# A fused RWKV and mixture-of-experts block: products of ones at the start, first rows on two queues, later lookups and more buffers for results

## The chip, the core and the metric

The kernel runs on one core of a Trainium2 chip. A core has a matrix engine (PE), a vector engine (DVE), a scalar engine (ACT), a general engine (POOL), and a queue of its own for transfers (SP). ACT and POOL can start transfers too. Each engine takes its instructions strictly in program order and waits on semaphores for what the others produce; the on-chip memory has 128 partitions. The metric is the device time in microseconds (us) of one execution, as a median of several.

## The reference

Input is `x` of shape (2, 2048, 256). What is computed, all in float32:

```
xn  = layernorm(x)                                  # over the last axis, 256 wide
# attention: a decaying sum over time, per channel
k, v = xn @ key_w.T, xn @ value_w.T                 # k does not enter the recurrence
r    = sigmoid(xn @ recep_w.T)
att  = (r * wkv_scan(time_decay, time_first, v)) @ out_w.T
# mixture of experts: 8 experts, the best 2 of each row, and one shared expert
scores = softmax(xn @ gate_w.T + gate_b);  top 2 of 8
expert(e) = (silu(xn @ w1[e].T + b1[e]) * (xn @ w3[e].T + b3[e])) @ w2[e].T + b2[e]
y = sum over the two experts of a row of score * expert
z = (silu(xn @ ws1.T + bs1) * (xn @ ws3.T + bs3)) @ ws2.T + bs2   # shared, 512 wide inside
out = x + att + y + z
```

There are 4096 rows, so 8192 pairs of a row and an expert.

## The kernel before

The 4096 rows are 8 chunks of 512 rows, each of 4 groups of 128. Chunks are taken in the order `ORDER` = 2, 3, 0, 1, 4 (`FIRST`), then 5, 6, 7 (`LAST`). The work has four stages.

1. **Rows in.** `load_flow` (L428) issues on SP the rows of each chunk, the weights `ws13` of the shared expert in two halves (after the first and third chunk, `WHEN`), and then the other weights. `norm_flow` (L485) normalizes: statistics on DVE (L495, L497), the power on POOL (L500, L501), then the even groups on DVE (L507), the odd ones with a shift from DVE (L511) on ACT (L515). `turn_flow` (L519) transposes the rows on PE (L530), ACT copies them out, and PE makes the gate scores (L552, L562).
2. **Routing.** `route_flow` (L578) finds on DVE the two experts of each row and the place of each pair in a sorted list. `scatter_flow` (L733) then writes the rows to `xs_d` in that order, with 64 indirect transfers on POOL (L744), paced by the products of PE.
3. **Experts.** The sorted list is 66 tiles of 128 pairs: 50 taken two at a time with one expert (`double_flow`, L1257), 7 single ones, and 9 mixed ones that hold up to four experts in quarters (`tile_flow`, L1169). Their order is `SEQ`, sorted from the numbers in `PLACE` (L210). `rows_flow` (L1131) loads the sorted rows on SP and transposes them on DVE. `goes_flow` (L1154) loads 2 numbers for each pair of 8 tiles from `xs_d` (`meta`, L1161) and makes of them, with two small DVE operations (L1165, L1166), the places `goes` to which the results belong. `store` (L1242) writes the results to `ys_d` by indirect transfers on POOL.
4. **Results back.** When all tiles are stored, `collect_flow` (L1320) loads for each group the two results of its rows (`y`, 32 loads of 256 KB on SP, three buffers), and `combine_flow` (L1331) adds them with their scores on DVE (L1338). The sums of a chunk start as `x` (`base_flow`, L965) plus the bias `bs2` (`bias_sum_flow`, L975, an add of 128x1024 on DVE at L980). `out_flow` (L1368) writes them out.

Beside these stages PE has work that can be put where there is room: the hidden layer of the shared expert (`hidden_flow`, L930, products at L951), the attention's projections (L883) and their last products (`dense_flow`, L1002, products at L1020). Hidden layers of the last chunks are held back (L935) and fill the time in which the results come back.

The order on every engine is written by a planner when the program is built (`Plan`, L84). Each flow is a generator that yields the engine and a length in ns that it asks for (`on`, L177), a pause, or an event to wait for. The planner takes the request that can start first; among those within 150 ns of each other on one engine, it takes the lower rank. `Room` counts free buffers: `U` is a pool of 32 buffers of 2 KB a partition (`NU`), `KEEP` and `MORE` are how many of them a hidden layer has to leave free, `X` three buffers for the sums, `Y` the three for `y`. `land` (L398) is the planner's model of a transfer. On the chip, the engines follow the planned order, whatever the real times are.

Of the kernel before, what the change touches and what calls it, by code (L numbers as in the profile page):

```python
# [208 lines left out]

PLACE = {j: j / 2 for j in range(0, DBL, 2)}  # L210
PLACE |= {j: 6.1 + 2.1 * (j - DBL) for j in range(DBL, UNI)}
PLACE |= {j: 5.5 + 2 * (j - UNI) for j in range(UNI, TILES)}
SEQ = sorted(PLACE, key=PLACE.get)
assert sorted(SEQ) == [*range(0, DBL, 2), *range(DBL, TILES)]
AT = {j: n for n, j in enumerate(SEQ)}
# [9 lines left out]

PIECES = (((0,), (1,), (2,), (3,)), ((0, 1), (2, 3)))
NU = 32
KEEP = 3

FIRST, LAST = (2, 3, 0, 1, 4), (5, 6, 7)  # L230
ORDER = FIRST + LAST

HALVES = [(FIRST[0], i) for i in range(2)]

WHEN = (0, 2)

PACE = 4000

# [1 line left out]

LATE = 1000

BETWEEN = (2, 4)

EAGER = 6
MORE = 8

AHEAD = [(LAST[0], i) for i in range(2)]

# [4 lines left out]
def rwkv_moe_kernel(  # L254
# [33 lines left out]
    ROWS, H, YS = Room(plan, 2), Room(plan, 3), Room(plan, 3)  # L288

    PH, HP, PO = (Room(plan, n) for n in (4, 2, 2))  # L290
    XST, SIS, HST, Y = Room(plan, 3), Room(plan, 2), Room(plan, 2), Room(plan, 3)

    STILL = Room(plan, 3)
    STATS, MIX, XSM = Room(plan, 3), Room(plan, 1), Room(plan, 1)
# [57 lines left out]
    goes = fixed([P, TILES], "goes", I32)  # L352

    def constants():
        make_identity(nc, ident)
        nc.gpsimd.memset(zero, 0.0)
        nc.gpsimd.memset(neg_half, -0.5)
        nc.gpsimd.memset(ones, 1.0)

        nc.gpsimd.memset(before, 1.0)  # L360
        nc.gpsimd.affine_select(
            out=before, in_=before, pattern=[[1, P]], compare_op=ALU.is_gt, fill=0.0, base=0, channel_multiplier=-1
        )

        for e in range(E):
            nc.gpsimd.memset(rev[:, e : e + 1], float(E - e))

        for q in range(P // Q):
            nc.gpsimd.iota(
                starts[ts(q, Q)], pattern=[[P, TILES]], base=q * Q, channel_multiplier=0,  # L370
                allow_small_or_imprecise_dtypes=True,
            )
        nc.gpsimd.memset(wg[:, :, E:], 0.0)
        nc.gpsimd.memset(st_pp, -10000.0)
        nc.gpsimd.memset(st_bb, 0.0)
        nc.gpsimd.memset(st_aa, 0.0)


    loaded = {}
    have = {n: event() for n in ("vec", "wg", ("ws13", 0), ("ws13", 1), "ws2", "bs2", "wa", "x", "cleared", "we", "bias_d", "bias", "routed", "tiles")}  # L380
    normed = {(c, n): event() for c in range(NCH) for n in range(NT)}
    turned = {c: event() for c in range(NCH)}
    half_turned = [event() for _ in range(2)]
# [14 lines left out]
    def land(nbytes, then, *rooms):  # L398


        def flow():
            yield on(nbytes / 370, "Q")
            yield 2000
            for e in then:
                e.set()
            for r in rooms:
                r.give()

        plan.add(flow(), 0)

    def number_flow(c):
# [3 lines left out]
            allow_small_or_imprecise_dtypes=True,  # L415
        )

    def small_load_flow():

        for to, of in (  # L420
            (vec, vecs), (bg, b_gate.partition_broadcast(P)),
            (wg[:, :, :E], w_gate.rearrange("p (k e) -> p k e", k=NC)),
        ):
            yield on(600, "ACT")
            nc.scalar.dma_start(to, of)
        land(P * (NV * 4 + 64), [have["vec"], have["wg"]])

    def load_flow():  # L428
        for i, c in enumerate(ORDER):
            side = "left" if c in LEFT else "right"  # L430
            xn[c] = p_early[side].tile([P, NT, R], F32, tag=f"xn{c}", name=f"xn_{c}")
            for groups in PIECES[i > 0]:
                n, m = groups[0], len(groups)
                yield on(300 + 100 * m, "SP")
                nc.sync.dma_start(xn[c][:, n : n + m, :C], rows(x, c)[:, n : n + m, :])
                loaded[c, n] = event()
                plan.add(norm_flow(c, groups), 1 + i / 10)
                land(P * m * C * 4, [loaded[c, n]])
            plan.add(number_flow(c), 2)
            if i in WHEN:  # L440
                n = WHEN.index(i)
                of = slice(n * SI // 2, (n + 1) * SI // 2)
                yield on(600, "SP")
                nc.sync.dma_start(
                    ws13[:, :, :, of], w_sh13.rearrange("p (m k i) -> p m k i", m=2, k=NC)[:, :, :, of]
                )
                land(P * 4096, [have["ws13", n]])
        land(0, [have["x"]])
        yield on(500, "SP")
        nc.sync.dma_start(ws2, w_sh2.rearrange("p (k d) -> p k d", k=NSI))  # L450
        land(P * 4096, [have["ws2"]])
        yield on(500, "SP")
        nc.sync.dma_start(bs2, b_out[E, :].partition_broadcast(P))
        land(P * 1024, [have["bs2"]])
        for n, name in enumerate(("wv", "wr", "wo")):
            yield on(500, "SP")
            nc.sync.dma_start(wa[name], w_attn[n].rearrange("p (k d) -> p k d", k=NC))
        land(3 * P * 2048, [have["wa"]])

# [273 lines left out]
    def scatter_flow():  # L733
# [4 lines left out]
        for side, chunks in (("left", LEFT), ("right", RIGHT)):  # L738
# [27 lines left out]
        yield LATE  # L766
# [4 lines left out]
            flow = still_flow if j < DBL else one_flow if j < UNI else quarters_flow  # L771
            plan.add(flow(j), (9 if j < DBL else 15) + AT[j] / 100)
        for j in range(0, TILES, GO):
            plan.add(goes_flow(j), 10 + j / 100)
        plan.add(collect_flow(), 3)


# [152 lines left out]
    def hidden_flow(c, i):  # L930

        if (c, i) not in HALVES:
            yield turned[c]
        yield have["ws13", i // 2]
        if c in LAST and (c, i) not in AHEAD:  # L935
            yield turn[SEQ[-6]]
        pts = []
# [37 lines left out]
    def bias_sum_flow(c):  # L975
        t = sums[c]
        yield have["bs2"]
        yield have["routed"]
        yield on(1250, "DVE")
        nc.vector.tensor_tensor(  # L980
            t, t, bs2.unsqueeze(1).to_broadcast([P, NT, C]), ALU.add
        )
        sum_ready[c].set()
# [147 lines left out]
    def rows_flow(j):  # L1131
# [19 lines left out]
        turned_rows[j] = xT  # L1151
        rows_in[j].set()

    def goes_flow(j):  # L1154

        for c in range(NCH):
            yield scattered[c]
        n = min(GO, TILES - j)
        yield on(400, "SP")
        where = xs_d[j * P : (j + n) * P, R_TO:].rearrange("(n p) c -> p n c", p=P)  # L1160
        nc.sync.dma_start(meta[:, j : j + n, :], where)  # L1161
        yield 4000
        yield on(320, "DVE")
        to, top = meta[:, j : j + n, 0], meta[:, j : j + n, 1]
        nc.vector.tensor_tensor(top, top, likes[:, j : j + n], ALU.is_equal)  # L1165
# [154 lines left out]
    def collect_flow():  # L1320

        yield have["tiles"]
        for c in DONE:
            for n in range(NT):
                g = c * NT + n
                yield on(420, "SP", (Y, 1))
                y = late["ys"].tile([P, 2, C], F32, tag="ys", name=f"y_{g}")
                nc.sync.dma_start(y, ys_d[2 * g * P : 2 * (g + 1) * P, :].rearrange("(p w) c -> p w c", w=2))
                plan.add(combine_flow(c, n, y), 4)

    def combine_flow(c, n, y):  # L1331
# [1 line left out]
        yield 2000  # L1333
        yield sum_ready[c] if c in LAST else resumed[c]
        g = c * NT + n
        yield on(960, "DVE")
        for w in range(2):
            nc.vector.scalar_tensor_tensor(  # L1338
                sums[c][:, n, :], y[:, 1 - w, :], score[w][:, g : g + 1], sums[c][:, n, :], ALU.mult, ALU.add
            )  # L1340
        Y.give()
        step_done(c, n, closing[c, n // 2])

    def step_done(c, n, done):
# [40 lines left out]
            closing[c, half] = {"pe": pe, "sum": 0, "of": 2 + (c in LAST), "then": leaves(c, half)}  # L1385

    constants()
    plan.add(small_load_flow(), 0)
    plan.add(load_flow(), 0)
    for i, c in enumerate(ORDER):  # L1390
        plan.add(turn_flow(c), 1 + i / 10)
        if c in FIRST:
# [101 lines left out]
```

## Time and profile before

| | |
|---|---|
| median of 3 runs | 470.21 us (469.22 to 470.86) |
| the profiled execution | 469.83 us, of which the span is 468.1 us |
| mean granted clock of PE in the profiled execution | 0.992 |
| DVE, ACT, POOL busy | 360.5 us (77%), 195.4 us (42%), 192.4 us (41%) |
| loads of `y`, of `meta`, indirect stores to `ys_d` | 32, 9, 66 |

The span runs from the first to the last instruction of the program; 1.7 us lie around it. "Busy" counts the time in which an instruction of the engine is under way. For PE the page says itself that the ends of products are modelled and that a busy PE is not PE at its peak. The lists in order of time have start, length, engine, line, operation, output and inputs, how many instructions were merged, and in brackets the idle time ahead with what ended it.

### The profile page before, as it was taken

The page shows a single profiled execution, that of the slowest core. Times are in us where ns is not written, and L with a number is a line of the kernel's source. Part 1 is how long each engine was busy: PE and PEld are TensorE (multiplying, and loading weights), DVE is VectorE, ACT ScalarE, POOL GpSimd, SP SyncE. Part 2 cuts the span into 40 slices and gives each one's busy share as a digit, 9 for nine tenths or more (in the row PEclk, how much of TensorE's full clock was granted, in tenths as well). Part 3 has the DMA queues.
Part 4 walks back from the last instruction along what each step waited for, and adds up shares of the span by engine and source line. Part 5 has one row for each costly group of instructions (what it writes and reads, how often), then busy time and mean ns, then how long its engine had stood idle before and what let it go on. Part 6 is the DMA issues. An engine that isn't in the chain of part 4 may idle for free.

```text
span 468.1 us, 6776 instructions
## 1 busy us (share of the span) xinstructions
PE 449.2 (96%) x1965; PEld 295.2 (63%) x1965; DVE 360.5 (77%) x722; ACT 195.4 (42%) x383; POOL 192.4 (41%) x228
## 2 busy tenths in 40 slices
PE   4999999999999988999999999999999999999994
PEld 2755556444686556866676656667667576445883
DVE  4776999979678468986897789476559777786876
ACT  3777210261140316436934683734877245112000
POOL 6650047777777012365435444464452432200000
PEclk9999999999999998999999999999999999999998
DMA  7999922475253885477736585666685400278885
GB/s 230 365 269 193 281 73 82 139 243 182 102 177 109 225 159 153 153 205 215 177 106 193 166 235 168 194 163 201 175 263 135 151 17 34 91 215 297 264 286 174
DMA packets 90980, 84.93 MB, mean 181 GB/s; under 512 B 50429, under 2 KB 76318, under 8 KB 90816
## 3 DMA queue, kind: packets, MB, share of 16 engines
q1 hardware_dynamic: 82432, 62.24, 47.2%
q0 software_dynamic: 7952, 22.23, 15.2%
q8 instruction: 16, 0.26, 0.2%
q14 instruction: 20, 0.16, 0.1%
q10 hardware_dynamic: 560, 0.04, 0.1%
HBM read 44.93 MB, written 26.70 MB: 153 GB/s over the span
## 4 chain that ended last, share of the span: by engine, by line
PE 72%; DVE 11%; DMA 10%; SPq 3%; issue 3%; DVEq 0%; ACT 0%
PE ph L1285 16%; PE p L951 15%; PE pos L1308 9%; PE po L1020 9%; DMA y<-ys_d 6%; PE wvp L883 6%; PE wrp L883 4%; PE ph L1183 3%; PE ph L1187 3%; DVE pa L1338 2%; PE pos L1225 2%; PE tp L530 2%; DVE si L960 1%; DMA xs<-xs_d 1%; SPq L1143 1%
## 5 line engine op out<-in xcount | busy, mean ns | idle before, releaser
L1247 POOL DMA_INDIRECT ys_d<-ys,goes x66 | 75.6, 1146 | 141.1 <-DVE ys L1315 45.0
L951 PE MATMUL p<-xnT,ws 128*128 128x512 f32 (+1 forms) x272 | 116.7, 576 | 0.0
L1285 PE MATMUL ph<-xsT,still 128*128 128x256 f32 x400 | 93.3, 381 | 0.9 <-DMA xs<-xs_d 0.9
L744 POOL DMA_INDIRECT xs_d<-xn,slot x64 | 68.8, 1075 | 49.1 <-DVE eq L690 29.9
L951 PEld LDWEIGHTS p<-xnT,ws 128*128 128x128 f32 x272 | 51.9, 195 | 53.2 <-issue 49.6
L1285 PEld LDWEIGHTS ph<-xsT,still 128*128 128x128 f32 x400 | 74.7, 190 | 14.8 <-issue 5.2
L1020 PE MATMUL po<-ws,si 128*128 128x256 f32 x256 | 59.3, 379 | 1.1 <-DVE si L960 1.1
L1020 PEld LDWEIGHTS po<-ws,si 128*128 128x128 f32 x256 | 48.6, 190 | 11.1 <-issue 2.6
L1308 PE MATMUL pos<-we,si 128*128 x200 | 50.0, 395 | 3.3 <-DVE si L1298 2.1
L1308 PEld LDWEIGHTS pos<-we,si 128*128 128x128 f32 x200 | 37.8, 195 | 19.7 <-issue 5.6
L957 ACT ACTIVATE si<-p,vec 128x512 f32<-128x512 f32 x32 | 21.7, 685 | 56.3 <-PE p L951 56.2
L1119 ACT COPY own<-we 128x512 f32 x72 | 40.2, 621 | 1.0 <-issue 0.9
L1147 DVE STREAM_TRANSPOSE xsT<-xs 128x512 f32<-128x512 f32 (+1 forms) x41 | 24.5, 600 | 16.7 <-DMA xs<-xs_d 15.7
L911 ACT ACTIVATE th<-wrp 128x512 f32<-128x512 f32 x16 | 9.5, 596 | 66.3 <-PE wrp L883 61.8
L1271 ACT ACTIVATE si<-ph,bcol 128x256 f32<-128x256 f32 x50 | 21.0, 471 | 32.4 <-PE ph L1285 30.3
L1298 DVE SCALAR_TENSOR_TENSOR si<-ph,bcol,si 128x256 f32<-128x256 f32 x50 | 21.6, 473 | 15.1 <-PE ph L1285 14.6
L1020 PE MATMUL po<-wo,rw 128*128 128x256 f32 x128 | 31.9, 379 | 0.0
L883 PE MATMUL wrp<-xnT,wr 128*128 128x512 f32 x64 | 30.1, 592 | 0.0
L883 PE MATMUL wvp<-xnT,wv 128*128 128x512 f32 x64 | 29.1, 595 | 0.0
L1020 PEld LDWEIGHTS po<-wo,rw 128*128 128x128 f32 x128 | 24.3, 190 | 5.0 <-issue 1.9
L864 DVE RECIPROCAL bb<-bb 128x512 f32<-128x512 f32 x8 | 26.8, 3353 | 0.3
L1315 DVE TENSOR_TENSOR ys<-pos,b 128x512 f32<-128x512 f32 x25 | 17.2, 686 | 12.1 <-PE pos L1308 11.7
(158 smaller groups left out, 592.5 us busy)
## 6 DMA issues: line engine op xcount, KB each, us to landing
still<-we SPq DMA_DIRECT2D x25, 512.0 KB
y<-ys_d SPq DMA_DIRECT2D x32, 256.0 KB
xs<-xs_d SPq DMA_DIRECT2D x100, 64.0 KB
we<-in_w_exp_dram SPq DMA_DIRECT2D x16, 256.0 KB
xb<-in_x_dram SPq DMA_DIRECT2D x8, 512.0 KB
pa<-part_d SPq DMA_DIRECT2D x8, 512.0 KB
xn<-in_x_dram SPq DMA_DIRECT2D x14, 256.0 KB
part_d<-xb SPq DMA_DIRECT2D x5, 512.0 KB
```

The costliest lines, as they stand in the source:

```text
L744: step = nc.gpsimd.indirect_dma_start(out=xs_views[2 * g + w], out_offset=bass.IndirectOffsetOnAxis(ap=slot[w][:, g : g + 1], axis=0), in_ ...
L864: nc.vector.reciprocal(den, den)
L883: nc.tensor.matmul(pt, wa[name][:, k, ts(ch, P)], xnT[c][k], start=(k == 0), stop=(k == NC - 1))
L951: nc.tensor.matmul(pts[m][:, of], ws13[:, m, k, ts(i, P)], xnT[c][k][:, of], start=(k == 0), stop=(k == NC - 1))
L957: nc.scalar.activation(si, pts[0], AF.Silu, bias=vec[:, V_BS1 + i : V_BS1 + i + 1])
L1020: nc.tensor.matmul(po[:, j, :], l[:, ts(2 * half + j, P)], r, start=(i == 0), stop=(i == len(parts) - 1))
L1119: nc.scalar.copy(mine[q, k], we[:, which[j, q], 0:2, k, :])
L1147: nc.vector.transpose(xT.rearrange("p k (b t) -> p b k t", t=Q), t.rearrange("p b (k i) -> p b k i", i=Q))
L1247: nc.gpsimd.indirect_dma_start(out=ys_views[j], out_offset=bass.IndirectOffsetOnAxis(ap=goes[:, j : j + 1], axis=0), in_=y, in_offset=None ...
L1285: nc.tensor.matmul(p[m][:, i, :], mine[k][:, m, ts(i, P)], xT[:, k, :], start=(k == 0), stop=(k == NC - 1))
L1298: nc.vector.scalar_tensor_tensor(si[:, i, :], p[1][:, i, :], mine["b"][:, 1, i : i + 1], si[:, i, :], ALU.add, ALU.mult)
L1308: nc.tensor.matmul(po[:, t, :], si[:, i, ts(t, P)], we[:, e, 2, i, :], start=(i == 0), stop=(i == NI - 1))
```

## The change

The changed places are named after what they do. Before the first rows arrive, PE multiplies a tile of ones by itself 20 times (`warm_flow`). Of the first chunk's rows, groups 1 and 3 are issued from ACT ahead of the small loads, groups 0 and 2 from SP. `ws13` comes in quarters: after the first chunk, after the second, and two after the third. The planner's model of a transfer goes from 370 bytes per ns and 2000 ns to 330 and 2200. `goes_flow` waits for a tile that lies `SOON` = 8 tiles ahead of the first that needs the lookup, if there is such a tile, and leaves 8000 instead of 4000 ns for the transfer. The bias sums of chunks 2, 3, 5, 6, 7 go from DVE to POOL, and those of 2 and 3 no longer wait for the routing. `y` has five buffers instead of three, taken from the pool `U`, and its adds have rank 45 instead of 4. `KEEP`, `BETWEEN`, `EAGER` and `PLACE` get other numbers.

```diff
-PLACE |= {j: 5.5 + 2 * (j - UNI) for j in range(UNI, TILES)}
+PLACE |= {j: 5 + 2 * (j - UNI) for j in range(UNI, TILES)}
...
-KEEP = 3
+KEEP = 2
...
-WHEN = (0, 2)
+WHEN = (0, 1, 2, 2)
...
-BETWEEN = (2, 4)
-EAGER = 6
+BETWEEN = (2,)
+EAGER = 7
...
+ASIDE = FIRST[:2] + LAST
+WARM = 20
+SOON = 8
+BACK = 5
...
-    XST, SIS, HST, Y = Room(plan, 3), Room(plan, 2), Room(plan, 2), Room(plan, 3)
+    XST, SIS, HST, Y = Room(plan, 3), Room(plan, 2), Room(plan, 2), Room(plan, BACK)
...
     def constants():
+        nc.gpsimd.memset(ones, 1.0)
         make_identity(nc, ident)
...
-        nc.gpsimd.memset(ones, 1.0)
...
-            yield on(nbytes / 370, "Q")
-            yield 2000
+            yield on(nbytes / 330, "Q")
+            yield 2200
...
+    def x_load(engine, c, groups, i):
+        n, m = groups[0], len(groups)
+        engine.dma_start(xn[c][:, n : n + m, :C], rows(x, c)[:, n : n + m, :])
+        loaded[c, n] = event()
+        plan.add(norm_flow(c, groups), 1 + i / 10 + n / 100)
+        land(P * m * C * 4, [loaded[c, n]])
+
+    def warm_flow():
+        yield 600
+        yield on(3800, "PE", (PS, 1))
+        t = bank([P, P], "warm")
+        for n in range(WARM):
+            nc.tensor.matmul(t, ones, ones, start=True, stop=True)
+        PS.give()
+
     def small_load_flow():
+        for n in range(1, NT, 2):
+            yield on(450, "ACT")
+            x_load(nc.scalar, ORDER[0], (n,), 0)
...
             for groups in PIECES[i > 0]:
-                n, m = groups[0], len(groups)
-                yield on(300 + 100 * m, "SP")
-                nc.sync.dma_start(xn[c][:, n : n + m, :C], rows(x, c)[:, n : n + m, :])
-                loaded[c, n] = event()
-                plan.add(norm_flow(c, groups), 1 + i / 10)
-                land(P * m * C * 4, [loaded[c, n]])
+                if i or groups[0] % 2 == 0:
+                    yield on(400 + 75 * len(groups), "SP")
+                    x_load(nc.sync, c, groups, i)
             plan.add(number_flow(c), 2)
             if i in WHEN:
-                n = WHEN.index(i)
-                of = slice(n * SI // 2, (n + 1) * SI // 2)
+                n, m = WHEN.index(i), WHEN.count(i)
+                of = slice(n * P, (n + m) * P)
...
-            plan.add(goes_flow(j), 10 + j / 100)
+            plan.add(goes_flow(j), 10 + needed(j) / 100)
...
-        yield have["ws13", i // 2]
+        yield have["ws13", i]
...
         yield have["bs2"]
-        yield have["routed"]
-        yield on(1250, "DVE")
-        nc.vector.tensor_tensor(
+        aside = c in ASIDE
+        if not aside:
+            yield have["routed"]
+        yield on(*((2300, "POOL") if aside else (1250, "DVE")))
+        (nc.gpsimd if aside else nc.vector).tensor_tensor(
             t, t, bs2.unsqueeze(1).to_broadcast([P, NT, C]), ALU.add
         )
...
+    def needed(j):
+        return min(AT[i if i in AT else i - 1] for i in range(j, min(j + GO, TILES)))
+
     def goes_flow(j):
...
+        if needed(j) >= SOON:
+            yield turn[SEQ[needed(j) - SOON]]
...
-        yield 4000
+        yield 8000
...
-                yield on(420, "SP", (Y, 1))
-                y = late["ys"].tile([P, 2, C], F32, tag="ys", name=f"y_{g}")
+                yield on(420, "SP", (Y, 1), (U, 1))
+                y = u([P, 2, C], f"y_{g}")
...
-        yield on(960, "DVE")
+        yield on(960, "DVE", rank=45)
...
         Y.give()
+        U.give()
...
+    rows_tile(ORDER[0])
+    plan.add(warm_flow(), 0)
+    plan.add(load_flow(), 0)
     plan.add(small_load_flow(), 0)
-    plan.add(load_flow(), 0)
```

(`rows_tile` makes the tile `xn` of a chunk, as `load_flow` did.)

More of the change, by code (lines that the diff above doesn't have):

```diff
@@ L379, in rwkv_moe_kernel @@
     loaded = {}
-    have = {n: event() for n in ("vec", "wg", ("ws13", 0), ("ws13", 1), "ws2", "bs2", "wa", "x", "cleared", "we", "bias_d", "bias", "routed", "tiles")}
+    have = {n: event() for n in ("vec", "wg", *(("ws13", i) for i in range(NSI)), "ws2", "bs2", "wa", "x", "cleared", "we", "bias_d", "bias", "routed", "tiles")}
     normed = {(c, n): event() for c in range(NCH) for n in range(NT)}
@@ L416, in number_flow, with rows_tile @@
         )
+    def rows_tile(c):
+        side = "left" if c in LEFT else "right"
+        xn[c] = p_early[side].tile([P, NT, R], F32, tag=f"xn{c}", name=f"xn_{c}")
+    def x_load(engine, c, groups, i):
[11 more added lines that the diff above has]
+        PS.give()
     def small_load_flow():
+        for n in range(1, NT, 2):
+            yield on(450, "ACT")
+            x_load(nc.scalar, ORDER[0], (n,), 0)
         for to, of in (
@@ L429, in load_flow @@
         for i, c in enumerate(ORDER):
-            side = "left" if c in LEFT else "right"
-            xn[c] = p_early[side].tile([P, NT, R], F32, tag=f"xn{c}", name=f"xn_{c}")
+            if i:
+                rows_tile(c)
             for groups in PIECES[i > 0]:
-                n, m = groups[0], len(groups)
-                yield on(300 + 100 * m, "SP")
-                nc.sync.dma_start(xn[c][:, n : n + m, :C], rows(x, c)[:, n : n + m, :])
-                loaded[c, n] = event()
-                plan.add(norm_flow(c, groups), 1 + i / 10)
-                land(P * m * C * 4, [loaded[c, n]])
+                if i or groups[0] % 2 == 0:
+                    yield on(400 + 75 * len(groups), "SP")
+                    x_load(nc.sync, c, groups, i)
             plan.add(number_flow(c), 2)
             if i in WHEN:
-                n = WHEN.index(i)
-                of = slice(n * SI // 2, (n + 1) * SI // 2)
+                n, m = WHEN.index(i), WHEN.count(i)
+                of = slice(n * P, (n + m) * P)
                 yield on(600, "SP")
@@ L446, in load_flow @@
                 )
-                land(P * 4096, [have["ws13", n]])
+                land(m * P * 2048, [have["ws13", n + q] for q in range(m)])
         land(0, [have["x"]])
```

## The prediction, made before the changed kernel was run

> **What bounds the kernel now.** The busy shares and the 40 slices of the page come first.
>
> ```profile
> PE 449.2 (96%) x1965; PEld 295.2 (63%) x1965; DVE 360.5 (77%) x722; ACT 195.4 (42%) x383; POOL 192.4 (41%) x228
> ...
> PE   4999999999999988999999999999999999999994
> ```
>
> PE is the bound: no other engine reaches 80%, and the chain that ended last is 72% PE. The products are the same after the change, so time can be won only where PE stands still or runs slowly: the low digits at the start, near slices 14 and 15 (164 to 187 us), and at the end. I read the order of time in those places.
>
> ```profile
> 5.68 0.69 PE L530 MATMUL tp<-ident,xn 128*128 128x128 f32 x2 [5.68 <-DVE xn L507]
> ...
> 8.38 2.07 PE L951 MATMUL p<-xnT,ws 128*128 128x256 f32 x4
> ...
> 18.90 1.89 PE L951 MATMUL p<-xnT,ws 128*128 128x256 f32 x8
> ```
>
> **Start.** PE begins at 5.68. Four 256-wide products take 2.07 us at 8.38, but eight take 1.89 at 18.90: 0.43 each against 0.215 (less some 0.17 for the last one's end). Full pace comes at about 12.9, after some 4.5 us of steady work, though the granted clock reads 1.00. The table of 2 us stretches gives 9.23 us of busy PE in the first 16 us. Idle are 6.8; the half pace costs 10 products x 0.215 = 2.1, and about 1.2 on the transposes. So 10.1 us are lost there.
>
> ```profile
> 9.05 0.75 DVE L495 BATCH_NORM_STATS2 stats<-xn 128x6 f32<-128x256 f32 x2 [1.95 <-DMA xn<-in_x_dram]
> 9.72 0.30 DVE L497 BATCH_NORM_AGGREGATE mv<-stats 128x2 f32<-128x6 f32 x2
> 9.94 0.12 DVE L511 SCALAR_TENSOR_TENSOR shift<-mv,rstd 128x1 f32<-128x1 f32 x1
> ```
>
> Here DVE waits 1.95 us for the second chunk's rows while the last shift of the first chunk, all of whose inputs are there, stands behind it; ACT and PE wait for that shift until 10.76.
>
> **First experts.** PE has run out of other work when the first tiles come.
>
> ```profile
> 166.03 0.17 DVE L1165 TENSOR_TENSOR meta<-meta,likes 128x8 f32<-128x8 f32 x1 [0.66 <-DMA meta<-xs_d]
> ...
> 167.66 1.97 PE L1308 MATMUL pos<-we,si 128*128 x8 [1.04 <-issue]
> ...
> 174.02 0.16 DVE L1165 TENSOR_TENSOR meta<-meta,likes 128x2 f32<-128x2 f32 x1 [0.98 <-issue]
> ...
> 176.94 3.63 PE L1308 MATMUL pos<-we,si 128*128 x8 [2.14 <-DVE si L1298]
> ```
>
> All nine lookups are issued between 158 and 170, and DVE takes them in line: it waits for their transfers and so reaches the product `si` (L1298) late, which PE needs. PE idles 1.04 and 2.14 there (and 0.87 at 161.21), and the eight products at 176.94 take 3.63 instead of 1.97: half pace again.
>
> **End.** The order of time, and SP's own waits:
>
> ```profile
> 460.29 1.03 PE L1020 MATMUL po<-wo,rw 128*128 128x256 f32 x4
> ...
> 462.82 2.60 SPq L1373 DMA_DIRECT2D out_dram<-xb  x3
> 463.24 1.00 DVE L1338 SCALAR_TENSOR_TENSOR xb<-y,score,xb 128x256 f32<-128x256 f32 x2 [0.45 <-DMA y<-ys_d]
> 464.16 0.75 DVE L1046 TENSOR_TENSOR xb<-po,xb 128x256 f32<-128x256 f32 x2
> ...
> SPq L1328 <- DVE pa L1338: 13.3, 13, 2.4
> ...
> SPq L1328 <- DMA y<-ys_d: 11.1, 8, 2.1
> ```
>
> PE ends at 461.32, but DVE works on a late `y` until 464.24 and closes at 464.91; 3.2 us later the span ends. SP waits 13.3 + 6.0 us (its two rows for adds that free a buffer) before loads of `y`. PE is unbroken from 405 to 461, so beyond PE's own end only the tail is to be had.
>
> **The change, part by part.**
>
> *Products of ones.* A float32 product is two records (272 records at L951 for 136 calls), so 20 calls are 40 records, 128 wide: half of 0.215, so 0.108 each at full pace and 0.215 at half. Ones are ready near 1.0, as POOL's first fills now take until 1.0. By the trace's 4.5 us the pace turns at 5.5 after 21 records; 19 more take 2.1: end at about 7.6. The Trainium skill (TensorE: Matmul & The Clock Gate, "What's actually happening") says the array is at half clock by default, that some 3.4 us of sustained work open it and one idle window of 3.4 us closes it. By this the ones end at 1.0 + 3.4 + 24 x 0.108 = 7.0. But the trace shows half pace after an idle of only 2.1 us (176.94), so I take its 4.5 us. Bounds: 7.0, and 9.6 if the gate opens only after all. Either way they overrun the first transposes (5.68 before), which is against the change: useful work starts 2 us later, but at full pace and with all four groups at hand.
>
> *First rows on two queues, quarters.* An issue takes 0.43 to 0.67 us on SP. Groups 1 and 3 and half of `ws13` leave the way of the second chunk's rows: two issues (0.9 us) and 256 KB less. The skill (DMA: Bandwidth & Descriptors, "Issuing engines are not separate DMA queues") says a second issuing engine saves only the issue time. So 0.9, and not twice the bandwidth; with the 256 KB at 250 GB/s (the stretch 6 to 8) another 1.0. The second chunk's rows come near 7.5, the last shift near 8.5. PE then has products of the first half to do. The ACT queue's small loads follow 0.9 us later; the gate weights are first used at 13.96. With ones until 7.6 and 0.7 for ACT's copies ahead of the first real products, about 8.2 us are lost instead of 10.1: **-2.0** (0 to -3.5).
>
> This stays only if the routing comes earlier as well, because PE has little other work left when the scatter ends at 151. Routing starts on DVE at 41.8, behind the norms, and DVE's waits of 1.95 and 1.66 in the first 16 us shrink, so I keep it.
>
> *Lookups ahead.* Of nine groups only those of tiles 0, 8 and 56 are needed within 8 tiles (numbers in `SEQ` 0, 4, 6); 48 follows at once, five much later. On DVE some 5 x 0.34 = 1.7 us and waits of up to 2.5 us (0.25 + 0.66 + 0.65 + 0.98) leave this stretch. The stall at 166 (1.2 from its last product's end) can go, the one at 174 shrink from 2.1 to about 0.5, and the half pace (1.7) with it: 4.5 at most. If the pace still falls, 2.7. I take **-4.0**, nearer the first, since idles of 0.87 and 1.04 in this stretch cost no pace. The moved lookups are issued in SP's line among loads of tiles; their DMA waits are covered by 8 tiles of some 4.5 us each. DVE works on them when PE has a full line: nothing. For the new wait, the tile named has been turned long before, and it is the planner's only.
>
> *`PLACE`.* Mixed tiles move from half numbers to whole ones, which doubles have too. The sort keeps the order of entry at equal numbers, doubles first: the sequence is the same. Nothing.
>
> *Bias sums on POOL.* One costs DVE 1.22 (L980: eight of 1.18 to 1.22). The trace has no such add on POOL. From below a fill of 128x1032 there (0.96 at L462); from above the skill (GPSIMD Engine Reference, "Engine selection"), which advises against it: two-input adds are some 2 times slower than on DVE, so 2.4. I take 2.4. In the tail POOL is idle, so no cost: DVE loses 3 x 1.22 = 3.7 us. By the rule on the path they would cost 3 x 1.2 = 3.5 more. The two early ones are the danger: POOL is in order, `xb` of chunks 2 and 3 is issued at 22.3 and transfers then take some 5.65 us (second chunk's rows), while the powers of the last chunks (L500) still run until 33. Two sums ahead of them could hold these norms 0 to 8 us. The planner expects the data earlier, and ranks the sums last. **+1.0.**
>
> *Five buffers.* If all `y` and their adds were done when PE ends, the closing add would end at 461.32 + 0.1 + 0.37 = 461.8, and 3.2 more give 465.0: -3.1 at most, 0 at least. The `y` loads take 54.6 us for 31 steps; 3 us are 5%, and the waits for buffers were 19. The transfers stand at 0.94 busy in 450 to 460 but 0.73 in 440 to 450, so there is room for 5%. With DVE's 3.7 us: **-2.8**. `U` has 5 fewer for hidden layers, which must leave 8; I reckon one of them moves behind a product of chunk 5, with others to fill.
>
> *`KEEP`, `BETWEEN`, `EAGER`, the planner's model* only reorder. I cannot price the new order: 0, with -2 to +3 in the range.
>
> Sum: -2.0 - 4.0 + 1.0 - 2.8 = -7.8. On the profiled execution's 469.83 that is 462.0. The median shown lies 0.4 higher, so **462.3**.
>
> **The rivals.**
>
> *Half of it is given back.* PE gets its early work done sooner, but the scatter (64 x 1.375 us on POOL) ends when it did; the start's gain becomes idle time before the first experts; the pace still falls there (2.7), and transfers hold the tail to 1.5. Then 469.8 - 2.7 - 1.5 + 1.0 = 466.6, or 467.0 as a median. For it: PE's idles at 160 to 177. Against: the norms' own waits shrink.
>
> *Slower: the early bias sums hold the powers.* POOL waits for `xb` until about 28, sums until 33, and the four powers due from 26.6 on come late; routing, scatter and experts slip by up to 8 us, and PE has nothing to put there. The start's gain is gone: 469.8 + 8 - 4.0 - 2.8 = 471.0, or 471.4. It decides from a slip of 6.8 on. For it: the 5.65 us of those transfers. Against: `xb` for the first two is issued early, and two of eight chunks are late at most.
>
> *It doesn't do what it says.* The ones end at 9.6 and cost what they win, the stalls at the first experts move to another product, `y` is bound by the transfers: 470.
>
> **How the numbers follow.** Forecast 0.58 (459 to 465), given back 0.24 (465 to 468.5), slower 0.11 (470.5 to 475), nothing 0.07 (469 to 471). 0.3% is 1.4 us, about what a measurement of this kernel can tell from no change. Of "nothing" I put 0.05 within it and 0.01 on each side: faster 0.83, same 0.05, slower 0.12. The range 458 to 469 leaves out the slower side and half of a tenth below.
>
> **What would show it.** Ones in PE from 1 to 7.6 and the first 256-wide products at 0.215; three or four lookups before the first expert's product, no idle over 1 us and no half pace there; the L980 sums on POOL before the scatter, with the last power still before 34; the end 3.7 us behind PE's last product. A last power after 36, or a first expert's product not before 161, would make me wrong.

## The result, and the profile after

The changed kernel took **477.0 us** (median of 9 runs, 472.38 to 479.21) against 470.06 us before (9 runs, 469.18 to 471.28): a ratio of 1.0147 [1.0114, 1.018]. It is slower by 1.5%, where 462.3 us was forecast. The profiled execution took 479.21 us, with a span of 477.5 us and a mean granted clock of 0.983. In a later set of runs it took 475.63 us beside 470.44. Executions more than 1.5% above the fastest of their kernel are left out of the ratios and medians below.

The busy shares, the slices and the shares of the chain, from the page of the changed kernel:

```profile
PE 455.3 (95%) x2005; PEld 299.9 (63%) x2005; DVE 360.8 (76%) x717; ACT 195.5 (41%) x383; POOL 204.9 (43%) x233
...
PE   8956999999999989998999997999999999999995
...
PE 68%; DMA 14%; DVE 11%; issue 3%; POOL 2%; SPq 1%; DVEq 0%; ACT 0%; POOLq 0%
```

The first digit has risen from 4 to 8. Part of that is work on ones: PE's 455.3 us contain 6.3 of it. But there is a new hole in the third and fourth slices (24 to 48 us), where every digit was 9, and POOL, which had no share of the chain before, now has 2% of it. A small hole lies in slice 25 (287 to 298 us); a second trace of the changed kernel doesn't have it, so it belongs to this execution and not to the change. The lines of this kernel have moved: the norms' powers are L528 and L529, hidden layers L978, transposes L558, bias sums L1010, base loads L997.

The start, in order of time on PE:

```profile
1.05 6.28 PE L443 MATMUL warm<-ones 128*128 128x128 f32 x40 [1.05 <-POOL ones L363]
7.17 0.60 PE L558 MATMUL tp<-ident,xn 128*128 128x128 f32 x4
8.12 1.13 PE L978 MATMUL p<-xnT,ws 128*128 128x256 f32 x4 [0.35 <-ACT xnT L565]
```

The ones end at 7.3, and the first four 256-wide products take 1.13 us instead of 2.07. That is as forecast. The hole is read on POOL:

```profile
22.81 0.72 POOL L529 TENSOR_TENSOR rstd<-rstd,neg_half 128x2 f32<-128x2 f32 x1
34.19 2.34 POOL L1010 TENSOR_TENSOR xb<-xb,bs 128x1024 f32<-128x1024 f32 x1 [10.67 <-DMA xb<-in_x_dram]
36.50 0.22 POOL L528 TENSOR_SCALAR rstd<-mv 128x2 f32<-128x2 f32 x1
36.80 0.71 POOL L529 TENSOR_TENSOR rstd<-rstd,neg_half 128x2 f32<-128x2 f32 x1
37.52 2.34 POOL L1010 TENSOR_TENSOR xb<-xb,bs 128x1024 f32<-128x1024 f32 x1
...
43.03 0.79 POOL L529 TENSOR_TENSOR rstd<-rstd,neg_half 128x2 f32<-128x2 f32 x1
```

POOL stands for 10.67 us in front of the first early bias sum. The next power, which needs nothing but statistics, comes after that sum, at 36.50. The second sum stands between that power and the last three, and the last one runs at 43.03. It ran at 32.55 before. The chain of waits shows what POOL waited for (start, length, what), and PE what came of it:

```profile
24.14 9.92 DMA xb<-in_x_dram
...
34.20 2.33 POOL xb L1010
```

```profile
30.37 0.64 PE L580 MATMUL by_e<-xnT,wg 128*32 128x128 f32 x16
40.11 1.49 PE L558 MATMUL tp<-ident,xn 128*128 128x128 f32 x4 [9.10 <-issue]
41.40 3.62 PE L978 MATMUL p<-xnT,ws 128*128 128x512 f32 x4
```

The load is issued at 24.14 and takes 9.92 us. PE idles for 9.10 us, and then works at half pace: 3.62 us for four 512-wide products that take 1.88 at 28.55, and 1.49 for four transposes that take 0.6 to 0.66. Routing begins at 54.3 us (before: 41.8), the scatter runs from 76.9 (63.1), the experts' products from 175.0 (161.2). The tail is shorter: PE's last group of products starts at 471.56 and ends at 472.6, and the span ends 4.9 us later; before, 6.8 us. So 14 us are lost ahead of the experts, and some of it comes back.

The half pace behind this hole stands in the granted clock as well, unlike that at the start of the kernel before, where the clock read 1.00 (columns: length; busy time and instructions of PE, PEld, DVE, ACT, POOL; granted clock, DMA share, GB/s). The clock is 0.68 of full speed in the mean of this stretch, where the kernel before has 1.00:

```profile
30.00:46.00 16.00, 6.75 (x35) 3.56 (x34) 6.93 (x20) 2.72 (x6) 8.43 (x10) 0.68 1.14 197
```

Not all of the 9.10 us is the wait for the transfer. The power of 36.80 lets DVE normalize a group, and this runs beside the second sum on POOL. Two such normalizations on DVE, the held one and a later one:

```profile
37.54 2.47 DVE L535 TENSOR_SCALAR xn<-xn,mv,rstd 128x256 f32<-128x256 f32 x1 [9.36 <-POOL rstd L529]
...
42.49 0.38 DVE L535 TENSOR_SCALAR xn<-xn,mv,rstd 128x256 f32<-128x256 f32 x1
```

The first takes 2.47 us instead of 0.38 and ends at 40.01, just behind POOL's sum (39.86); PE's transposes at 40.11 follow it. So some 2 us of the idle come from DVE being slow beside the sum.

### The profile page after: what moved, and what is told of

Same layout as the page of the kernel before. It is cut to its first block, busy times and chain, and to the rows that moved or that the text cites. A ratio compares the mean times of both kernels' runs of the same rounds, so it can differ in the third digit from the quotient of the medians.

```text
span 477.5 us, 6857 instructions
## 1 busy us (share of the span) xinstructions
PE 455.3 (95%) x2005; PEld 299.9 (63%) x2005; DVE 360.8 (76%) x717; ACT 195.5 (41%) x383; POOL 204.9 (43%) x233
## 4 chain that ended last, share of the span: by engine, by line
PE 68%; DMA 14%; DVE 11%; issue 3%; POOL 2%; SPq 1%; DVEq 0%; ACT 0%; POOLq 0%
PE ph L1321 15%; PE p L978 14%; PE po L1050 10%; PE pos L1344 9%; PE wrp L910 5%; PE wvp L910 4%; DMA y<-ys_d 4%; PE ph L1219 3%; PE ph L1223 2%; DMA xb<-in_x_dram 2%; DVE xb L1374 2%; DMA xn<-in_x_dram 2%; PE pos L1261 2%; DVE pa L1374 1%; POOL xb L1010 1%
## 5 line engine op out<-in xcount | busy, mean ns | idle before, releaser
L978 PE MATMUL p<-xnT,ws 128*128 128x512 f32 (+1 forms) x272 | 116.7, 575 | 0.4 <-ACT xnT L565 0.4
L978 PEld LDWEIGHTS p<-xnT,ws 128*128 128x128 f32 x272 | 51.0, 192 | 53.5 <-issue 48.6
L1010 POOL TENSOR_TENSOR xb<-xb,bs 128x1024 f32<-128x1024 f32 x5 | 11.7, 2347 | 53.6 <-DMA y<-ys_d 37.1
L987 DVE SCALAR_TENSOR_TENSOR si<-p,vec,si 128x512 f32<-128x512 f32 x32 | 23.6, 745 | 6.6 <-PE p L978 3.6
```

The lines of the kernel that those rows point to most:

```text
L978: nc.tensor.matmul(pts[m][:, of], ws13[:, m, k, ts(i, P)], xnT[c][k][:, of], start=(k == 0), stop=(k == NC - 1))
L987: nc.vector.scalar_tensor_tensor(si, pts[1], vec[:, V_BS3 + i : V_BS3 + i + 1], si, ALU.add, ALU.mult)
```

## The experiments

The theory after the result (A in the expectations): POOL, in its written order, waits for `xb` and holds the last norms, and this costs about 11.6 us (9.1 idle, 1.7 + 0.8 of half pace). The rivals: the hold only moves idle time, so that another part of the change is to blame; or the new order of work costs (B), in the tail above all (D); or the sums on POOL cost by slowing DVE beside them (C).

**Four first edits.** In the first two, the early sums of the changed kernel go back to DVE, or are offered to the planner later. In the other two, bias sums go to POOL in the kernel before.

```diff
 # early sums on DVE
-ASIDE = FIRST[:2] + LAST
+ASIDE = LAST
 # early sums on POOL, later
-        yield 3500
+        yield 25000 if c in FIRST[:2] else 3500
 # kernel before: five sums on POOL (or only those of LAST)
-        yield have["routed"]
-        yield on(1250, "DVE")
-        nc.vector.tensor_tensor(
+        aside = c in FIRST[:2] + LAST
+        if not aside:
+            yield have["routed"]
+        yield on(*((2300, "POOL") if aside else (1250, "DVE")))
+        (nc.gpsimd if aside else nc.vector).tensor_tensor(
```

> The changed kernel with the bias sums of chunks 2 and 3 back on DVE behind the routing (ASIDE = LAST); all else as changed. Theory A (POOL, in order, waits at 24 to 34 us for the transfer of x and holds the norms' powers behind it): PE's idle of 9.1 us at 31 to 40 us and the half pace behind it go, the last power ends before 35 us, routing starts near 40 instead of 58; 460 to 466 us. Theory B (the new order of work, from EAGER, KEEP, the transfer model or the later lookups, is what costs): no gain beyond 2 us, 474 to 478.

> The changed kernel with one number changed: the planner's pause between the load of x and the bias sum of chunks 2 and 3 is 25000 instead of 3500 ns, so that both sums stay on POOL but stand behind the last power. Theory A: as good as the kernel with these sums on DVE, within 2 us, 460 to 466. Theory B: 474 to 478. Theory C (the sums themselves cost, by their 2.35 us each on POOL or by slowing DVE beside them): stays above 470, and DVE's instructions beside the sums are longer than elsewhere.

> The kernel before with nothing but the move of the five bias sums to POOL, the two early ones without the wait for the routing. Theory A: the hold shows in the old order as well, powers after 35 us and a PE idle of several us before 45; 474 to 482. Theory B: no idle, 467 to 471.

> The kernel before with the bias sums of chunks 5, 6 and 7 alone moved to POOL. Both theories: no hold early; DVE has 3.7 us less to do in the tail. 467.5 to 470.5; under 469 would mean that DVE's line in the tail was worth something by itself, 470 that the transfers of y set the tail.

The first two sets of runs were made on one chip, the third on another, each with runs of the kernel before beside it. In this first set the kernel before took 475.4 us (470.8 to 477.4), some 5 more than in every other set, and no run shows why. So the ratios count, as far as that slowness hit both kernels alike.

| kernel | us | ratio to before | routing from | experts from | PE's last product starts | span |
|---|---|---|---|---|---|---|
| early sums on DVE | 475.83 | 1.0022 [1.0001, 1.0043] | 40.3 | 165.2 | 461.9 | 473.1 |
| early sums later | 478.83 | 1.0096 [1.0068, 1.0124] | 43.2 | 166.7 | 464.2 | 474.5 |
| before, five sums on POOL | 500.37 | 1.0544 [1.0436, 1.0651] | 53.2 | 176.2 | 495.5 | 499.4 |
| before, late sums on POOL | 481.19 | 1.0146 [1.0068, 1.0223] | 42.2 | 165.8 | 464.0 | 474.9 |

In the first two the hold is gone and the routing is early, and yet both miss theory A's 460 to 466; the first lands in theory B's range. The marks of C came true in the second: it stays above 470, and beside the sums an operation of DVE on 128x2 takes 2.24 us instead of 0.16. But the first has no early sum on POOL and is little better. The last two are slower than any theory had said. The third shows the hold in a kernel with nothing else of the change (first fence: POOL), and a second wait at the other end (second fence: PE):

```profile
31.44 2.34 POOL L982 TENSOR_TENSOR xb<-xb,bs 128x1024 f32<-128x1024 f32 x1 [5.66 <-DMA xb<-in_x_dram]
```

```profile
473.32 1.22 PE L1022 MATMUL po<-wo,rw 128*128 128x256 f32 x2 [16.22 <-DVE rw L925]
```

POOL's 5.66 us and two sums of 2.34 put the routing 11.5 us later; the 16.22 us are another matter, DVE working on `y` before the last attention block. These four edits change requests that the planner sees, and it writes another order for every engine. With early sums on DVE, the eight reciprocals of the attention run at 70 to 415 us instead of 71 to 393, and 20 records of projections run after 400 us, where the kernel before has 8. SP's own waits of that kernel show one in the tail:

```profile
SPq L1410 <- DVE pa L1374: 23.8, 7, 13.3
```

One store waits 13.3 us for the adds on DVE, with the loads of `y` queued behind it, and 11.2 us lie between PE's last product and the end of the span. These runs show that the hold is real and can be removed. They don't show what it is worth, because the order changed with it.

**Both kernels, and two edits of the tail, on the same chip.** Rank 45 lets other work on DVE go ahead of the adds of `y`. On top of "early sums on DVE", one edit takes the rank away, and one gives `y` back its three own buffers as well.

```diff
 # rank as before
-        yield on(960, "DVE", rank=45)
+        yield on(960, "DVE")
 # and the buffers as before
-BACK = 5
+BACK = 3
...
-                yield on(420, "SP", (Y, 1), (U, 1))
-                y = u([P, 2, C], f"y_{g}")
+                yield on(420, "SP", (Y, 1))
+                y = late["ys"].tile([P, 2, C], F32, tag="ys", name=f"y_{g}")
...
-        U.give()
```

> The kernel before, unchanged, for its trace on the chip of the runs beside it[...]. Expected where it differs from the first profile: a slower scatter or slower loads of y, not slower products.

> The changed kernel beside the two below on one chip. Theory A: PE idle of about 9 us from 31 on, and slower than the kernel with the early sums on DVE by what that idle and the half pace behind it do not give back, 6 to 12 us. Theory B: within 2 us of it.

> Early sums on DVE (ASIDE = LAST), and the adds of y back at rank 4 instead of 45; five buffers from U stay. Theory D (in the tail the late rank puts the adds behind the attention on DVE, the stores of out wait for them in SP's line, and the loads of y stand behind the stores): no stretch of 10 us with the transfers under 0.3 busy between the first and the last y, the last y at least 4 us earlier after the first; 3 to 6 us faster than with rank 45. Theory E (the transfers set the tail): within 1.5 us of it.

> Early sums on DVE, and results back wholly as before: three buffers of their own, rank 4. Theory D: as good as five buffers with rank 4 or up to 3 us slower (three buffers), and faster than five with rank 45. Theory E: like both. If it is the fastest of the three, five buffers from U cost something of their own.

Before: 470.26 in the traced run, 470.44 as the median of seven others. On the same chip it is 5 us faster than in the first set, so its trace can't show what was slow there. Changed: 475.63, ratio 1.0126 [1.0089, 1.0163]; its trace has PE idle for 8.23 us and the same half pace, routing at 54.1 and the experts from 175.0. Against "early sums on DVE" it is level by the times (475.63 and 475.83) and 1.0% slower by the ratios, so this pair decides nothing between A and B. The edits of the tail took 487.86 (1.038 [1.0327, 1.0434]) and 487.98 (1.0391 [1.034, 1.0442]). Theory D had 3 to 6 us faster. The rank does not cost, it earns: between this kernel with it and without it lie 2.5% by the times, 3.6% by the ratios. The kernel with the old rank, on PE and then on DVE:

```profile
436.55 0.59 PE L1050 MATMUL po<-wo,rw 128*128 128x256 f32 x2
459.94 1.22 PE L1050 MATMUL po<-wo,rw 128*128 128x256 f32 x2 [22.80 <-DVE aa L924]
```

```profile
434.07 9.54 DVE L1374 SCALAR_TENSOR_TENSOR xb<-y,score,xb 128x256 f32<-128x256 f32 x16
...
447.20 3.35 DVE L891 RECIPROCAL bb<-bb 128x512 f32<-128x512 f32 x1
```

Sixteen adds of `y` go ahead of the last block of attention, and PE stands for 22.80 us. So D fell. Again the whole order had changed, so the size holds for this order only.

**Four edits that keep the order.** In the last set the planner gives every step the slot that it had in the changed kernel. Only the instructions of one step are emitted elsewhere or in another number. In the first, the two early sums are emitted after the last norm's power; PE, DVE, ACT and SP have the same instructions in the same order as the changed kernel. The other three build on that one.

```diff
 # POOL's order alone
-        (nc.gpsimd if aside else nc.vector).tensor_tensor(
-            t, t, bs2.unsqueeze(1).to_broadcast([P, NT, C]), ALU.add
-        )
+        def add():
+            (nc.gpsimd if aside else nc.vector).tensor_tensor(
+                t, t, bs2.unsqueeze(1).to_broadcast([P, NT, C]), ALU.add
+            )
+        if c in FIRST[:2]:
+            put_off.append(add)     # emitted in bias_rows_flow
+        else:
+            add()
 # and one product of ones
-        for n in range(WARM):
-            nc.tensor.matmul(t, ones, ones, start=True, stop=True)
+        nc.tensor.matmul(t, ones, ones, start=True, stop=True)
 # or: all nine lookups (loads, then sums) in the slots of the first
+        burst = [(i, min(GO, TILES - i)) for i in range(0, TILES, GO)] if j == 0 else []
 # or: three own buffers for y
-                y = u([P, 2, C], f"y_{g}")
+                y = late["ys"].tile([P, 2, C], F32, tag="ys", name=f"y_{g}")
```

> The changed kernel, in which only POOL's order differs: the two early bias sums stand behind the last norm's power instead of among the powers; every other engine has the same instructions in the same order. Theory A (POOL, in order, stands for xb and holds the last norms): no wait of POOL at 23 to 34 us, the last power before 35 us, PE without its idle of 8.4 to 9.1 us at 31 to 40 us and without the half pace behind it; the routing starts at 41 to 43 us instead of 54, the experts at 161 to 164 us; 463 to 466 us, 10 to 12 us below the changed kernel. Rival B (the hold only shifts idle time that the routing would have had anyway, and later stalls take it back): the routing starts earlier, but the end stays at 472 to 476 us.

> The kernel of the run beside it (early sums behind the last norm), with one product of ones in place of forty; all orders equal. If the ones bring full pace from the first product on (theory): the first products of 256 columns run at about half pace until some 12 us, and the time rises by 1.5 to 2.5 us. Rival (the loads and norms behind the first row set the start, so that the pace of the first products is hidden): within 0.5 us of the kernel beside it.

> The kernel with the early sums behind the last norm, in which all nine lookups of places are issued and computed together at the slot of the first one, as in the kernel before; the planned order of all else is kept. Forecast of the change's term: stalls and half pace of PE in the 20 us behind the first expert come back, 4 us slower. Rival (the nine small loads and sixteen small sums fit into idle time of SP and DVE, and the stalls there stand for rows and weights): within 1 us.

> The kernel with the early sums behind the last norm, in which the results come back through three buffers of their own instead of five shared ones; order kept. Forecast of the change's term: PE's last product starts at the same time, the end lies further behind it, 2 to 3 us slower. Rival (the rank of the adds, not the number of buffers, shortens the tail): within 1 us.

| kernel | us | ratio to before (470.56) | experts from | PE's last product starts | span |
|---|---|---|---|---|---|
| POOL's order alone | 464.33 | 0.9861 [0.9832, 0.9891] | 163.4 | 457.1 | 462.5 |
| and one product of ones | 464.09 | 0.9861 [0.9833, 0.9889] | 163.6 | 457.8 | 462.3 |
| and lookups in one burst | 469.5 | 0.9989 [0.9969, 1.0009] | 163.2 | 462.1 | 466.5 |
| and three buffers | 472.97 | 1.0086 [1.005, 1.0122] | 162.6 | 455.9 | 469.9 |

*POOL's order.* The first of these is the changed kernel with two instructions of POOL in another place, and it is 11.3 us faster (475.63 - 464.33). The changed kernel ran on the other chip; by the ratios it is 12.5. It beats both kernels, and 464.33 lies in theory A's 463 to 466. POOL, in order of time (bias sums are L1015 here):

```profile
31.77 0.79 POOL L529 TENSOR_TENSOR rstd<-rstd,neg_half 128x2 f32<-128x2 f32 x1
35.19 2.71 POOL L1015 TENSOR_TENSOR xb<-xb,bs 128x1024 f32<-128x1024 f32 x1 [2.62 <-DMA xb<-in_x_dram]
38.70 2.36 POOL L1015 TENSOR_TENSOR xb<-xb,bs 128x1024 f32<-128x1024 f32 x1 [0.81 <-DMA xb<-in_x_dram]
```

The transfer is as late as before (POOL still waits for it, until 35.19), but nothing is queued behind it now. The last power is done at 32.6. PE has no idle there and keeps its pace:

```profile
30.85 0.66 PE L558 MATMUL tp<-ident,xn 128*128 128x128 f32 x4
31.35 1.88 PE L982 MATMUL p<-xnT,ws 128*128 128x512 f32 x4
```

Routing comes 12.0 us earlier than in the changed kernel (42.3), the experts 11.6, the end 11.3. That agrees with the idle of 8.23 us in the second trace of the changed kernel plus 2.6 of half pace, 10.8. That the hold only moves idle time is refuted. So is C as the cause of the whole: the sums are still on POOL, and one still stretches an add on DVE (1.88 us instead of 0.68), but nothing on PE's way stands behind it now.

*Ones.* With a single one of the 20 products (2 of the 40 records) the time is the same (464.09). PE's start there, to be compared with the start shown above:

```profile
5.40 0.69 PE L557 MATMUL tp<-ident,xn 128*128 128x128 f32 x2 [3.56 <-DVE xn L534]
6.65 0.69 PE L557 MATMUL tp<-ident,xn 128*128 128x128 f32 x2 [0.56 <-ACT xn L542]
7.76 2.07 PE L981 MATMUL p<-xnT,ws 128*128 128x256 f32 x4 [0.42 <-ACT xnT L564]
```

The products run at half pace, but work begins 2 us sooner, as the prediction had noted against the ones. At 15 us this kernel is 0.5 us behind, when the experts begin 0.2, and at the end nothing of it is left. The rival was right, though its reason is the earlier start as much as the loads.

*Lookups.* Put into one burst, they cost 5.2 us. The burst kernel on SP (lookups are L1209), DVE and PE:

```profile
157.66 2.39 SPq L1183 DMA_DIRECT2D xs<-xs_d  x4
160.10 6.43 SPq L1209 DMA_DIRECT2D meta<-xs_d  x9
166.57 1.95 SPq L1183 DMA_DIRECT2D xs<-xs_d  x4
```

```profile
170.77 0.71 DVE L1187 STREAM_TRANSPOSE xsT<-xs 128x512 f32<-128x512 f32 x1 [7.05 <-DMA xs<-xs_d]
```

```profile
171.54 3.49 PE L1334 MATMUL ph<-xsT,still 128*128 128x256 f32 x8 [4.66 <-DVE xsT L1187]
```

Nine issues take SP 6.43 us, and the rows of the second tile are issued behind them. DVE waits 7.05 us for these rows, PE 4.66 for DVE, and then the next eight products run at half pace (3.49 instead of 1.89). The size is near the forecast, the way is not: DVE waits for rows, not for lookups. The stretch from 164 to 168 (columns as above) in the burst kernel and then in the one without it:

```profile
164.00:168.00 4.00, 2.88 (x14) 2.19 (x12) 0.00 (x0) 0.84 (x2) 0.00 (x0) 1.00 0.79 20
```

```profile
164.00:168.00 4.00, 4.00 (x20) 3.52 (x19) 3.93 (x8) 1.49 (x4) 0.00 (x0) 1.00 0.93 189
```

The DMA engines are busy for 0.79 of this stretch and move 20 GB/s; all but the last issues on SP in it are lookups. In the other kernel a load of 512 KB and rows fall into it. The kernel before had its nine as 1, 5, 1 and 2 with rows between them, not in one burst, so 5.2 us is not what the change saves.

*Buffers.* With three buffers in the order written for five, PE's last product starts 1.2 us sooner and the time is 8.6 us longer, where 2 to 3 were expected. SP's waits of this kernel (total, times, longest):

```profile
SPq L1374 <- DVE pa L1384: 19.8, 18, 4.1
...
SPq L1374 <- DVE xb L1384: 8.8, 8, 2.6
```

The 28.6 us in which the loads of `y` wait for adds are more than the 19.3 of the kernel before; with five buffers these rows do not appear among the twelve largest. DVE also waits for a late sum on POOL here, 2.65 us, but with five buffers it does so for 2.32 too:

```profile
451.12 1.92 DVE L1384 SCALAR_TENSOR_TENSOR xb<-y,score,xb 128x256 f32<-128x256 f32 x4 [2.65 <-POOL xb L1015]
```

The rank that holds the adds back needs the five buffers, so 8.6 us is not the gain over the kernel before either: there, 7.2 us (9.9 in its second trace) lie between the start of PE's last products and the end of the span, and 5.4 in the kernel with POOL's order mended.

## Why the prediction was wrong, step by step

**The step that failed** is the term of +1.0 for the two early bias sums, bounded by "0 to 8 us". The mechanism stood among the rivals, with a chance of 0.11 and a time of 471.4, and it was too small there too: a slip of up to 8 us, where the experts slipped 11.6 against the same order without the hold. The runs put the term at 11.3 us. Five parts of its working were off:

- The transfer. The term took 5.65 us for `xb`, from the second chunk's rows; it took 9.92. The row was measured on an early, short queue. Here the loads of `wr` and of other weights lie ahead; the DMA share by stretches is 1.09 from 16 to 30 us and 1.14 from 30 to 46, the highest of the run. The kernel before with early sums on POOL, whose `xb` is also issued near 22 us, waits until 31.4.
- The issue. The prediction used 22.3, the place in the order of before; in the changed order SP reaches it at 24.14.
- The sum of both: POOL is free again at 36.5 after the first sum, not at 33 after both.
- DVE beside the sum. The prediction put this at nothing. The normalization that the power at 36.80 had freed took 2.47 us instead of 0.4 beside the second sum (2.42 in the second trace), and PE stood for it.
- The half pace behind the idle. A slip of 8 us was priced as 8. An idle of that length also costs 1.7 us on the next products and 0.8 on the transposes, as the prediction itself had read at 176.94 and not applied here.

The argument against the rival, "`xb` for the first two is issued early", was the planner's view. With a model of a transfer that ends sooner than the real one, the planner puts the sums where they seem to wait for nothing; the chip follows the order, not the times.

**Start, -2.0: right at the place, lost on the way.** In the first 16 us the kernel with POOL's order mended has 14.24 us of busy PE, of which 6.50 are ones: 7.7 us of useful work at full pace, so 8.3 lost, where 8.2 was forecast. The ones have only a part in it: with one product of them 9.62 us are busy (10.41 less 0.79), of which half pace takes some 2.7 (1.6 on eight products, 1.1 on eight transposes, against the same ones with full pace), so 9.1 are lost. Of the 1.8 us, then, 1.0 comes from the rows and weights. Routing is no earlier than before (42.3 against 41.8); instead eight more records of hidden layers (2 x 1.88 us) are done ahead of the experts, which begin 2.2 us later.

**Lookups, -4.0: the stalls named are gone**, and a burst costs 5.2. But with POOL's order mended PE still idles 1.99 us at the first expert, and 0.82, 0.59 and 1.20 later, waiting for `si`. In the 60 us from PE's last work ahead of the experts it idles 4.6 us, and 4.1 in both traces of the kernel before. The half pace at 176.94, 1.7 of the 4.0, is missing in the second of these as well, so it was not there to be won in every execution.

**Bias sums in the tail, no cost: not shown.** They took 2.35 us in the mean, as the Trainium skill has it (GPSIMD Engine Reference, "Engine selection": two-input work some 2 times slower than on DVE, where it took 1.22), and far from the fill's 0.96. With POOL's order mended DVE stands 2.32 us at 445.68 for a sum on POOL; whether the end moves with it, no run shows. In the kernel before, late sums on POOL alone brought 1.0146, but in another order.

**Five buffers, -2.8: right in direction.** With POOL's order mended the tail gives 1.8 to 4.5 us, by the two traces of before.

**The sum.** Without its +1.0 the forecast is -8.8 us. The kernel with POOL's order mended measures -6.2 (470.56 to 464.33). So the other terms together were about 2.6 too hopeful. The stretches read above point to the lookups: 1.8 won at the start, 1.8 to 4.5 in the tail, and between 1.2 won and 0.5 lost at the first experts. That is an estimate between kernels of different order; no run separates these terms. The hold takes all of it back: with the 10.8 us read from the trace it is -6.2 + 10.8 = +4.6, and the changed kernel was +5.2 against the runs of before beside it. Of the marks set down, the ones and the full pace came true; the last power at 43.03 and the first expert's product at 175.0 were those that would make the forecast wrong.

## What to carry to other kernels

An instruction moved to another engine brings its wait along: ask what stands behind it in that engine's order, and price it with the transfer's time at that moment, under that load, not with a row from a quieter moment. Ask too what the old engine runs beside it. To learn what a step costs in a kernel whose order a planner writes, keep the order and move only the instructions; an edit that the planner sees changes all of it. Where full pace must be paid for with work on nothing, compare it with simply starting earlier at half pace.

## What the runs showed of the hardware

- In all traces from 16 us on, the pace of PE halved behind every idle of 2.66 us or more and behind one of 2.14, and behind none up to 1.99. Each time some 1.6 us or more were lost. Near 2.1 us the length does not decide it alone: an idle of 2.15 us in "before, late sums on POOL" left the pace whole (16 products in 3.69 us, as many as the kernel before does in 3.69 behind 0.87). The kernel before fell on both sides at one product: 3.63 us after an idle of 2.14 in its first trace, and in its second

```profile
175.93 1.97 PE L1308 MATMUL pos<-we,si 128*128 x8 [1.93 <-DVE si L1298]
```

  The mean granted clock from 155 to 200 us was 0.96 in the first and 1.00 in the second. The Trainium skill (TensorE: Matmul & The Clock Gate, "What's actually happening") puts the limit at an idle window of 3.4 us; here 2.14, 2.66, 3.20 and 3.24 us were enough.
- Some operations of DVE that ran beside a bias sum on POOL ended only with it: normalizations took 2.42 to 2.47 us instead of 0.38 to 0.41 in three traces, an add of 128x512 took 1.88 and 2.49 instead of 0.68 in two. Not all do: a `si` of a hidden layer (L991) took its usual 0.74 us inside the second early sum of the kernel with POOL's order mended.
- In a stretch of 4 us in which SP issued almost nothing but lookups, the DMA engines were busy for 0.79 of the time at 20 GB/s, against 0.93 at 189 GB/s in the other kernel, where a load of 512 KB and rows fall into it.
- On one chip the kernel before took 475.4 us in one set of runs and 470.4 in the next; on another it took 470.6. Ratios to runs made beside them were needed, and they are only as good as this drift allows.
